# A two-layer vision tower on one Trainium2 core: the order of work where layer 1's attention begins and ends

## The chip, the cores and the metric

The kernel runs on one core of one Trainium2 chip. The core has five engines that take their instructions in order [...]: TensorE (PE, matrix products; its weight loads are shown apart as PEld), VectorE (DVE), ScalarE (ACT), GpSimd (POOL) and SyncE (SP, which here only issues DMA). The metric is the device time of one execution in microseconds (us), the median of several runs.

## The reference, cut to what matters

32 images of 256 tokens with 256 features go through a tokenizer and two layers. Layer 0 is a gated attention and a feed-forward that works only on the 127 best-ranked tokens of each image; layer 1 is the attention that the change is about, and a feed-forward with experts. All is float32.

```
h = tokenizer(x)
h = h + attn0(layernorm(h))                    # stage B of the kernel
x = layernorm(h)                               # stage C
w = x @ wr + br;  idx = the 127 largest of w;  h = h + x
h[idx] += w[idx] * (gelu(x[idx] @ w1 + b1) @ w2 + b2)
x = layernorm(h)                               # stage D
k = tanh(gelu(x @ Wk1 + bk1) @ Wk2 + bk2) * freq * pi    # phases; q likewise
r[i] = sum over j <= i of sum over phases of cos(k[j] - q[i]) * (x[j] @ Wv + bv)
h = h + x + layernorm(r / sqrt(64 * (i + 1))) @ Wo + bo
h = h + ffn1(layernorm(h))                     # stage E
```

## The kernel before, in words

`H` holds all 32 images in on-chip memory, two blocks of 128 tokens each. Every engine's instructions run in exactly the order in which the program writes them: a manual schedule covers PE, DVE, ACT, POOL and SP. So the Python loops below *are* the queues, and an instruction that waits holds all that is written after it on its engine. All matrix products go to one pool of eight PSUM banks (`bank()`), taken in turn; a bank can be taken again when its reader of eight allocations ago is done.

**Stage B** (layer 0's attention) ends with a step that makes the norms and ranking weights of images 28 and 29 (`norms_c`), turns the first quad's ranked tokens (`turn_c(0)`) and writes the last output (`output_b`, PE's rows `w_wo,gT`).

**Stage C** (layer 0's feed-forward, from line 847) goes by quads of four images. `step_c(t)` reads a table, `ORDER_C`: for a quad whose turn it is, `hidden_c` in two halves (rows `xsel,w_w`; ACT applies the gelu), `made` in two halves (rows `w_w,hT`; DVE adds a bias into `cy`, SP writes it to `results` in DRAM), `turn_c` of the next quad, and then for the quad that is done `fetch` (POOL: four indirect DMAs from `results` into `cx`, half a quad at a time) and `update` (DVE: `h<-cx,w_kept,h` at line 827 with new statistics, then a power on POOL). Which tokens are ranked is found by `ranks`: PE turns the weights (`turn_weights`, row `ident,cw`, line 482), DVE compares every weight with every other (lines 389 to 397), and POOL scatters the tokens to `ranked` in DRAM by their rank. The rankings of the last four images fall in steps 0 and 1 of stage C. There, PE's first product of step 1 stands behind a turn of weights that need `norms_c(B-2)`, which on DVE is written after `ranks(B-4)`.

**Stage D** (layer 1's attention, from line 873) goes by pairs of images; a pair is named by its first image. Step r of pair u runs at `t = 3u + r`:

- 0 `norm_d` (DVE, into `dx`; the first pair's norms, in `cx`, are made ahead, in stage C),
- 1 `turn` (PE transposes, ACT and DVE copy one half each into `dxT`) and `residual_d` (POOL, four adds of 128x512),
- 2 `hidden` twice (PE rows `dxT,w_wk` and `dxT,w_wq`; ACT gelu into `dg`),
- 3 `phases` (PE rows `dg`; ACT tanh; a chain on DVE: `dz` twice, `dn`, `dz`; ACT `Sin`). Gelu and `Sin` need different function tables of ACT, so each change costs a table load,
- 4 `match` (PE rows `dz`; DVE multiplies by the causal weights into `dat`),
- 5 `memory` (PE rows `dat`; ACT copies into `dm`),
- 6 `output` (PE rows `wvo,dm`, four banks; DVE statistics of each; `pow_rstd` on POOL),
- 7 `add_output` (DVE, line 952, waits for that power and frees the four banks) and `stats_e` (DVE, then a power on POOL).

So in a full round three pairs are under way, and the latency of one pair's chain is covered by PE work of the others. In the first round there is no other pair yet, and in the last none any more. The last quad's `fetch` and `update` of stage C (`step_c(32)` to `step_c(34)`) are written into stage D at t = 3, 4 and 5.

**Stage E** (layer 1's feed-forward, line 983 on) is a pipeline over images with a table of its own; the change doesn't touch it.

Of the kernel before, what the change touches and what calls it, by code (L numbers as in the profile page):

```python
# [33 lines left out]
F32 = mybir.dt.float32  # L34
# [6 lines left out]
P = 128  # L41
B, N, D = 32, 256, 256
NC = N // P
# [36 lines left out]
def vit_tower(tc, a, out):  # L80

    nc = tc.nc
    top = ExitStack()
    cpool = top.enter_context(tc.tile_pool(name="cpool", bufs=1))
    spool = top.enter_context(tc.tile_pool(name="spool", bufs=3))
# [59 lines left out]
    def pow_rstd(o, var):  # L145

        n = o.shape[1]
        nc.gpsimd.tensor_scalar(o, var, 1.0, 1e-5, ALU.mult, ALU.add)
        nc.gpsimd.tensor_tensor(o, o, minus_half[:, 0:n], ALU.pow)
# [52 lines left out]
    px = passing_x.enter_context(tc.tile_pool(name="c_x", bufs=1, reuse_waits="tile"))  # L202
# [69 lines left out]
    with (  # L272
# [7 lines left out]
        for k, n in enumerate(PARTS):  # L280
            f = sum(PARTS[:k])
# [68 lines left out]
        for b in range(B):  # L350
# [12 lines left out]
            if b in (B - 6, B - 4):  # L363
                u = (b - B + 6) // 2
# [39 lines left out]
    with (  # L404
# [71 lines left out]
        def turn_weights(b0):  # L476
            p = bank()
            for j in range(2):
                w = normed_c[b0][j][1]
                for c in range(NC):  # L480
                    o = j * N + c * P
                    nc.tensor.transpose(p[:, o : o + P], w[:, c : c + 1].to_broadcast([P, P]), ident)  # L482
            return p

        def ranks(b0, p):
            for j in range(2):
                rank_c(b0 + j, *normed_c[b0][j], p[:, j * N : (j + 1) * N])
# [54 lines left out]
    p2 = region_c.enter_context(tc.tile_pool(name="c_2", bufs=2, reuse_waits="tile"))  # L542
# [224 lines left out]
    def norm_d(b0, s, pool, name, bufs):  # L767
        s.xs = []
        for j in range(2):
            x = pool.tile([P, NC, D], F32, name=name, bufs=bufs)  # L770
            st, rs, i = at(st_d, b0 + j)
            q = slice(i * NC, (i + 1) * NC)
            one = spool.tile([P, NC], F32, name="d_one")
            nc.vector.scalar_tensor_tensor(one, st[:, i, :, 0], -1.0, rs[:, q], ALU.mult, ALU.mult)
            nc.vector.tensor_scalar(one, one, 1.0, None, ALU.add)
            for c in range(NC):
                nc.vector.tensor_scalar(
                    x[:, c, :], H[b0 + j][:, c, :], rs[:, i * NC + c : i * NC + c + 1], one[:, c : c + 1],
                    ALU.mult, ALU.add,
                )  # L780
            s.xs.append(x)

    def residual_d(b0, s):
        for j in range(2):
            h = H[b0 + j]
            nc.gpsimd.tensor_tensor(h, h, s.xs[j], ALU.add)
            nc.gpsimd.tensor_tensor(h, h, over(add_row, [P, NC, D], 1), ALU.add)

    with region_c:
        st_d = new_stats("d")  # L790

        def hidden_c(b0, s, half):
            if half == 0:
                s.hT = p2.tile([P, 8, 4 * P], F32, name="hT")
            for m in range(4 * half, 4 * half + 4):
                p = bank()
                for k in range(2):
                    mm(p, w1[:, k, m * P : (m + 1) * P], s.xsel[:, k, :], k == 0, k == 1)
                nc.scalar.activation(s.hT[:, m, :], p, AF.Gelu_apprx_tanh, bias=col("b1", m))

        def made(b0, s, half):
            for j in range(2 * half, 2 * half + 2):
                p = bank()
                for m in range(8):
                    mm(p[:, 0:D], s.hT[:, m, j * P : (j + 1) * P], w2[:, m, :], m == 0, m == 7)
                y = p2.tile([P, D], F32, name="cy", bufs=4)
                nc.vector.tensor_tensor(y, p[:, 0:D], row_c("b2"), ALU.add)
                nc.sync.dma_start(results[b0 + j][:], y)

        def fetch(b0, s, half):  # L810
            s.y = s.y if half else []
            for b in range(b0 + 2 * half, b0 + 2 * half + 2):
                y = px.tile([P, NC, D], F32, name="cx", bufs=8)
                for c in range(NC):
                    k = b * NC + c
                    nc.gpsimd.indirect_dma_start(
                        y[:, c, :], None, results[b][:], bass.IndirectOffsetOnAxis(rank_of[:, k : k + 1], 0)
                    )
                s.y.append(y)

        def update(b0, s, half):
            for j in range(2 * half, 2 * half + 2):
                b = b0 + j
                st, rs, i = at(st_d, b)
                for c in range(NC):
                    k = b * NC + c
                    nc.vector.scalar_tensor_tensor(
                        H[b][:, c, :], s.y[j][:, c, :], w_kept[:, k : k + 1], H[b][:, c, :], ALU.mult, ALU.add
                    )
                    stats(st, i, c, H[b][:, c, :])  # L830
            pow_rstd_of(st_d, b0 + 2 * half, 2)

        ORDER_C = ((0, hidden_c, 0), (1, hidden_c, 1), (2, made, 0), (-1, turn_c, 0), (-8, first_ranks, 0),
                   (3, made, 1), (4, fetch, 0), (5, fetch, 1), (5, update, 0), (6, update, 1))

        def step_c(t):
            for at_step, do, j in ORDER_C:
                u, r = divmod(t - at_step, 4)  # L840
                if r == 0 and 0 <= u < B // 4 and (u > 1 or do is not first_ranks):
                    do(4 * u, quads[u], j)

        END_C = 4 * (B // 4 - 1) + 4
        pairs = [Pair() for _ in range(B // 2)]
        preparing = prepare()
        for t in range(END_C):
            if t < 2:
                ranks(B - 4 + 2 * t, turn_weights(B - 4 + 2 * t))
            if t == 0:  # L850
                norms_c(B - 2)
                residuals_c(B - 2)
            if t == END_C - 2:
                norm_d(0, pairs[0], px, "cx", 8)
            step_c(t)
            if t >= 8:
                next(preparing, None)
        passing.close()
# [5 lines left out]
    with (  # L864
# [3 lines left out]
        def turn(b0, s):  # L868
            s.xT = p2.tile([P, 2, 2 * N], F32, name="dxT")
            transposed(s.xT, s.xs, copy_split)  # L870

        def hidden(b0, s, i):

            g = p2.tile([P, 2, 2 * N], F32, name=f"dg{i}")
            for m in range(2):
                p = bank()
                for k in range(2):
                    mm(p, (wk1, wq1)[i][:, k, m * P : (m + 1) * P], s.xT[:, k, :], k == 0, k == 1)
                nc.scalar.activation(g[:, m, :], p, AF.Gelu, bias=bias_d[:, 2 * i + m : 2 * i + m + 1])
            s.g = (s.g if i else []) + [g]  # L880

        def phases(b0, s):

# [48 lines left out]
                nc.scalar.copy(m.rearrange("p k n -> p (k n)"), p)  # L932
                s.m.append(m)

        def output(b0, s):
            st_m = spool.tile([P, 2 * NC, 2], F32, name="d_st")
            s.po = []
            for q in range(2 * NC):
                m, c, p = s.m[q // NC], q % NC, bank()
                for k in range(2):  # L940
                    mm(p, m[:, k, c * P : (c + 1) * P], wvo[:, k, :], k == 0, k == 1)
                six = spool.tile([P, 6], F32, name="six")
                nc.vector.bn_stats(six, p[:, 0:D])
                nc.vector.bn_aggr(st_m[:, q, :], six)
                s.po.append(p)
            s.rs = spool.tile([P, 2 * NC], F32, name="d_rs")
            pow_rstd(s.rs, st_m[:, :, 1])

        def add_output(b0, s):
            for q, p in enumerate(s.po):  # L950
                h = H[b0 + q // NC][:, q % NC, :]
                nc.vector.scalar_tensor_tensor(h, p[:, D:], s.rs[:, q : q + 1], h, ALU.mult, ALU.add)
# [6 lines left out]

        for t in range(3 * (B // 2 - 1) + 8):
            def do(step, which, *more):
                u, r = divmod(t - step, 3)
                if r == 0 and 0 <= u < B // 2:
                    which(2 * u, pairs[u], *more)

            do(1, turn)
            do(7, add_output)
            if t != 4:  # L970
                do(4, match)
            do(7, stats_e)
            do(1, residual_d)
            do(2, hidden, 0)
            if t == 5:
                match(0, pairs[0])
            do(2, hidden, 1)
            do(5, memory)
            do(3, phases)
            if t:  # L980
                do(0, norm_d, p8, "dx", 4)
            do(6, output)
            if 3 <= t <= 5:
                step_c(END_C + t - 3)
    right_d.close()
    passing_x.close()
    by_hand.close()
# [721 lines left out]
```

## Time and profile before

| | |
|---|---|
| time | 2002.92 us, median of 3 runs (2000.7 to 2003.91) |
| span of the profiled execution | 2000.3 us, 37646 instructions |
| mean granted TensorE clock | 0.984 |
| stage C from its first hidden product to its last `made` | 692.0 to 933.9 us |
| stage D | 933.9 to 1285.0 us |
| a full round of stage D | 21.0 us |
| stage E | 1285.0 us to the end |

Times in the profile count from the span's start. In a timeline row the columns are start, duration, engine, line, operation, output and inputs, how many were merged, and in square brackets the idle time of the engine before it and what ended it. A line can be that of a helper: L115 is every matrix product, L188 the transposes in `transposed`, L482 the turn of the ranking weights. In a table by windows each stretch gives its length, the busy time of PE, PEld, DVE, ACT and POOL with their number of instructions, the granted clock of PE as a share of full speed, the share of DMA, and GB/s. A profile doubles some records of float32 products, so counts are read only against each other.

### The profile page before, as it was taken

The numbers are of one execution on the slowest core, as the hardware profiler recorded it, in microseconds if no ns is written. First come the engines' busy times: TensorE is split into PE (matmuls) and PEld (weight loads), VectorE is DVE, ScalarE is ACT, GpSimd is POOL, SyncE is SP. The second block draws the span as 40 slices with busy tenths as digits, with TensorE's granted clock in tenths as the row PEclk, the third lists the DMA queues.
The fourth block names the chain that finished last, engine by engine and source line by source line (L and its number), as shares of the span: only waits on it lengthen the run. The fifth ranks groups of instructions, "written<-read, shape, count | busy, mean of one in ns | idle before, by whom it ended". The sixth has DMA issues, their size and how long they took to land.

```text
span 2000.3 us, 37646 instructions
## 1 busy us (share of the span) xinstructions
PE 1942.6 (97%) x15108; PEld 1373.5 (69%) x15108; DVE 1289.7 (64%) x3605; ACT 824.6 (41%) x1549; POOL 722.7 (36%) x692
## 2 busy tenths in 40 slices
PE   9999999999999999998999999999999999999984
PEld 7886676666767666765555555577777777777762
DVE  2334566656565735334655646567889998989986
ACT  0002222222121111122344444377777777777761
POOL 1223234334342334234333342214443444444353
PEclk9999999999999999999999999999999999999995
DMA  8540000000000232121000000001222121212211
GB/s 297 158 142 1 0 19 29 24 14 22 11 21 11 85 98 80 52 68 50 11 1 1 0 1 1 6 18 44 49 53 57 44 65 44 60 49 58 52 50 54
DMA packets 69812, 95.08 MB, mean 48 GB/s; under 512 B 8576, under 2 KB 51200, under 8 KB 69248
## 3 DMA queue, kind: packets, MB, share of 16 engines
q1 hardware_dynamic: 62912, 75.04, 13.2%
q0 software_dynamic: 6144, 16.79, 2.7%
q8 instruction: 121, 1.98, 0.4%
q10 hardware_dynamic: 576, 0.79, 0.1%
q14 instruction: 59, 0.48, 0.1%
HBM read 46.45 MB, written 20.97 MB: 34 GB/s over the span
## 4 chain that ended last, share of the span: by engine, by line
PE 94%; DVE 4%; DMA 1%; ACT 0%; issue 0%; SPq 0%; POOL 0%; ACTq 0%; DVEq 0%
PE bank L115 89%; PE bank L750 2%; PE bank L188 1%; PE bank L1254 1%; DMA both<-hx 0%; DMA patch<-in_patches_dram 0%; PE bank L229 0%; PE bank L482 0%; DVE fout L1263 0%; DVE ctmp L375 0%; DVE two L1185 0%; DVE fout L1259 0%; DVE ctmp L391 0%; DVE ctmp L389 0%; DVE six L123 0%
## 5 line engine op out<-in xcount | busy, mean ns | idle before, releaser
L1102 ACT ACTIVATE et<-bank 128x512 f32<-128x512 f32 x384 | 202.4, 599 | 59.0 <-DVE bank L1100 58.5
L115 PEld LDWEIGHTS bank<-ev,et 128*64 128x64 f32 x6144 | 198.2, 137 | 33.2 <-ACT et L1102 20.6
L115 PE MATMUL bank<-ev,et 128*64 128x74 f32 (+1 forms) x6144 | 211.1, 226 | 0.0
L1100 DVE TENSOR_TENSOR bank<-bank,w_tri 128x256 f32<-128x256 f32 (+1 forms) x384 | 173.3, 514 | 56.1 <-PE bank L115 54.4
L1180 POOL TENSOR_TENSOR eo<-eo,gate 128x1024 f32<-128x1024 f32 x64 | 121.9, 1926 | 215.9 <-DVE gate L1177 203.2
L115 PE MATMUL bank<-g,sx 64*128 64x512 f32 (+1 forms) x512 | 191.0, 502 | 1.4 <-ACT g L1060 1.4
L115 PE MATMUL bank<-g,sw 64*128 64x512 f32 (+1 forms) x512 | 189.9, 502 | 0.1
L115 PE MATMUL bank<-tokW,patch 128*128 128x256 f32 x768 | 166.7, 380 | 2.8 <-DMA patch<-in_patches_dram 2.8
L115 PEld LDWEIGHTS bank<-tokW,patch 128*128 128x128 f32 x768 | 146.0, 190 | 23.8 <-DMA tokW<-in_tokW_dram 3.3
L115 PE MATMUL bank<-bxT,w_wuv 128*128 128x512 f32 x300 | 131.4, 592 | 0.0
L1132 POOL TENSOR_TENSOR hv<-hv,minus_half 128x8 f32<-128x8 f32 x64 | 119.5, 1868 | 5.3
L1118 ACT COPY eo<-bank 128x286 f32<-128x286 f32 x256 | 97.4, 423 | 57.9 <-PE bank L115 51.4
L115 PE MATMUL bank<-wvo,dm 128*128 128x512 f32 x256 | 114.0, 598 | 0.0
L115 PE MATMUL bank<-w_wo,gT 128*128 128x256 f32 x512 | 113.1, 379 | 0.0
L115 PE MATMUL bank<-xsel,w_w 128*128 128x512 f32 x256 | 113.1, 600 | 0.0
L115 PE MATMUL bank<-attn,bv 128*128 128x256 f32 x512 | 113.1, 379 | 0.0
L115 PE MATMUL bank<-w_w,hT 128*128 128x256 f32 x512 | 113.1, 379 | 0.0
L115 PEld LDWEIGHTS bank<-attn,bv 128*128 128x128 f32 x512 | 97.2, 190 | 19.6 <-issue 6.9
L123 DVE BATCH_NORM_STATS2 six<-h 128x6 f32<-128x256 f32 x256 | 105.5, 412 | 4.4
L1131 POOL TENSOR_SCALAR hv<-ranges 128x8 f32<-128x8 f32 x64 | 39.1, 611 | 190.1 <-DVE ranges L1193 189.9
L115 PEld LDWEIGHTS bank<-w_w,hT 128*128 128x128 f32 x512 | 96.7, 190 | 15.8 <-issue 3.4
L115 PEld LDWEIGHTS bank<-w_wo,gT 128*128 128x128 f32 x512 | 97.2, 190 | 13.2
(265 smaller groups left out, 3739.0 us busy)
## 6 DMA issues: line engine op xcount, KB each, us to landing
patch<-in_patches_dram SPq DMA_DIRECT2D x31, 768.0 KB
sw<-sx SPq DMA_DIRECT2D x64, 128.0 KB
both<-fxT SPq DMA_DIRECT2D x64, 128.0 KB
both<-hx SPq DMA_DIRECT2D x64, 128.0 KB
out_dram<-fout SPq DMA_DIRECT2D x32, 256.0 KB
cs<-ranked SPq DMA_DIRECT2D x32, 128.0 KB
results<-cy SPq DMA_DIRECT2D x32, 128.0 KB
w_w<-in_w_dram SPq DMA_DIRECT2D x2, 1024.0 KB
```

The source lines that it names most:

```text
L115: nc.tensor.matmul(o, lhsT, rhs, start=first, stop=last)
L123: nc.vector.bn_stats(six, x)
L188: nc.tensor.transpose(p[:, o : o + P], x[:, c, k * P : (k + 1) * P], ident)
L750: nc.tensor.transpose(p[:, o : o + P], x[:, c, k * P : (k + 1) * P], ident)
L1100: nc.vector.tensor_tensor(own, own, over(tri, [P, n_e, P], 1), ALU.add)
L1102: nc.scalar.activation(t, p, AF.Exp)
L1118: nc.scalar.copy(im.o[:, c * NH + n, 0:OC], p[:, 0:OC])
L1131: nc.gpsimd.tensor_scalar(v, x, 1.0 / HD, 1e-8, ALU.mult, ALU.add)
L1132: nc.gpsimd.tensor_tensor(v, v, minus_half, ALU.pow)
L1180: nc.gpsimd.tensor_tensor(im.mix[k], im.mix[k], over(im.gate[:, :, 2 * k : 2 * k + 2], [P, NC * NH, 2, HD], 3), ALU.mult)
L1254: nc.tensor.transpose(im.po[:, o : o + P], im.fT[:, k, c * P : (c + 1) * P], ident)
```

## The change

Three edits of order, at three places; no instruction is added or taken away.

1. *Rankings of the last four images.* In steps 0 and 1 of stage C the feed-forward's products (`step_c`) are written ahead of `ranks` and its turn of weights, so that PE has work while DVE makes norms and rankings.
2. *The start of layer 1's attention.* The second pair's `norm_d` is made together with the first's, in stage C, and its `turn` right after the first pair's hidden layers (t = 2). The first `match` moves between the two halves of the second pair's second hidden layer, so that it comes later on PE. The second pair's residual adds move to t = 5, and the last quad's `fetch` and `update` from t = 3, 4, 5 to t = 6, 7, 8.
3. *The end of layer 1's attention.* At t = 48 only three of the four products of the last but one pair's `output` are written; the last pair's `match` follows, then the fourth product and `add_output`. So the last `dat` stands ahead of the fourth statistics and of `add_output` on DVE, and PE has a product to do while DVE makes it.

```diff
         for t in range(END_C):
-            if t < 2:
-                ranks(B - 4 + 2 * t, turn_weights(B - 4 + 2 * t))
             if t == 0:
                 norms_c(B - 2)
                 residuals_c(B - 2)
             if t == END_C - 2:
-                norm_d(0, pairs[0], px, "cx", 8)
+                for u in range(2):
+                    norm_d(2 * u, pairs[u], px, "cx", 8)
             step_c(t)
+            if t < 2:
+                ranks(B - 4 + 2 * t, turn_weights(B - 4 + 2 * t))
...
-        for t in range(3 * (B // 2 - 1) + 8):
+        NP = B // 2
+        for t in range(3 * (NP - 1) + 8):
...
-            do(1, turn)
-            do(7, add_output)
+            last = t == 3 * NP + 1
+            if t != 4:
+                do(1, turn)
+            if not last:
+                do(7, add_output)
             if t != 4:
                 do(4, match)
+            if last:
+                output(B - 4, pairs[NP - 2], (3,))
+                add_output(B - 4, pairs[NP - 2])
             do(7, stats_e)
-            do(1, residual_d)
+            if t != 4:
+                do(1, residual_d)
             do(2, hidden, 0)
-            if t == 5:
+            if t == 2:
+                do(2, hidden, 1)
+                turn(2, pairs[1])
+            elif t == 5:
+                do(2, hidden, 1, (0,))
                 match(0, pairs[0])
-            do(2, hidden, 1)
+                do(2, hidden, 1, (1,))
+            else:
+                do(2, hidden, 1)
             do(5, memory)
             do(3, phases)
-            if t:
+            if t == 5:
+                residual_d(2, pairs[1])
+            if t > 3:
                 do(0, norm_d, p8, "dx", 4)
-            do(6, output)
-            if 3 <= t <= 5:
-                step_c(END_C + t - 3)
+            if t == 3 * NP:
+                output(B - 4, pairs[NP - 2], (0, 1, 2))
+            else:
+                do(6, output)
+            if 6 <= t <= 8:
+                step_c(END_C + t - 6)
```

`hidden` and `output` take a list of the parts to write, so that one call can be split in two.

More of the change, by code (lines that the diff above doesn't have):

```diff
@@ L870, in turn, with hidden @@
             transposed(s.xT, s.xs, copy_split)
-        def hidden(b0, s, i):
-            g = p2.tile([P, 2, 2 * N], F32, name=f"dg{i}")
-            for m in range(2):
+        def hidden(b0, s, i, ms=(0, 1)):
+            if ms[0] == 0:
+                s.g = (s.g if i else []) + [p2.tile([P, 2, 2 * N], F32, name=f"dg{i}")]
+            g = s.g[i]
+            for m in ms:
                 p = bank()
@@ L879, in hidden @@
                 nc.scalar.activation(g[:, m, :], p, AF.Gelu, bias=bias_d[:, 2 * i + m : 2 * i + m + 1])
-            s.g = (s.g if i else []) + [g]
         def phases(b0, s):
@@ L933, in memory, with output @@
                 s.m.append(m)
[L935 to L938, printed above, removed]
+        def output(b0, s, qs=range(2 * NC)):
+            if qs[0] == 0:
+                s.st, s.po = spool.tile([P, 2 * NC, 2], F32, name="d_st"), []
+            for q in qs:
                 m, c, p = s.m[q // NC], q % NC, bank()
@@ L943, in output @@
                 nc.vector.bn_stats(six, p[:, 0:D])
-                nc.vector.bn_aggr(st_m[:, q, :], six)
+                nc.vector.bn_aggr(s.st[:, q, :], six)
                 s.po.append(p)
-            s.rs = spool.tile([P, 2 * NC], F32, name="d_rs")
-            pow_rstd(s.rs, st_m[:, :, 1])
+            if len(s.po) == 2 * NC:
+                s.rs = spool.tile([P, 2 * NC], F32, name="d_rs")
+                pow_rstd(s.rs, s.st[:, :, 1])
         def add_output(b0, s):
@@ L958, in stats_e @@
             pow_rstd_of(st_e, b0, 2)
-        for t in range(3 * (B // 2 - 1) + 8):
+        NP = B // 2
+        for t in range(3 * (NP - 1) + 8):
             def do(step, which, *more):
                 u, r = divmod(t - step, 3)
-                if r == 0 and 0 <= u < B // 2:
+                if r == 0 and 0 <= u < NP:
                     which(2 * u, pairs[u], *more)
-            do(1, turn)
-            do(7, add_output)
+            last = t == 3 * NP + 1
[3 more added lines that the diff above has]
+                do(7, add_output)
             if t != 4:
                 do(4, match)
+            if last:
+                output(B - 4, pairs[NP - 2], (3,))
+                add_output(B - 4, pairs[NP - 2])
             do(7, stats_e)
-            do(1, residual_d)
+            if t != 4:
+                do(1, residual_d)
             do(2, hidden, 0)
-            if t == 5:
+            if t == 2:
[3 more added lines that the diff above has]
+                do(2, hidden, 1, (0,))
                 match(0, pairs[0])
-            do(2, hidden, 1)
+                do(2, hidden, 1, (1,))
+            else:
+                do(2, hidden, 1)
             do(5, memory)
             do(3, phases)
-            if t:
+            if t == 5:
+                residual_d(2, pairs[1])
+            if t > 3:
                 do(0, norm_d, p8, "dx", 4)
-            do(6, output)
-            if 3 <= t <= 5:
-                step_c(END_C + t - 3)
+            if t == 3 * NP:
[4 more added lines that the diff above has]
+                step_c(END_C + t - 6)
     right_d.close()
```

## The prediction

> **What bounds the kernel now.** I read the engine totals and the chain of the page first, then the chain in order of time around the third part of the span, then the windows and the timelines of PE, POOL and DVE there. Engine totals and chain shares:
>
> ```profile
> PE 1942.6 (97%) x15108; PEld 1373.5 (69%) x15108; DVE 1289.7 (64%) x3605; ACT 824.6 (41%) x1549; POOL 722.7 (36%) x692
> ...
> PE 94%; DVE 4%; DMA 1%; ACT 0%; issue 0%; SPq 0%; POOL 0%; ACTq 0%; DVEq 0%
> ```
>
> TensorE bounds it, so an edit pays only where PE stands still. The windows say where (PE busy, then the others, granted clock, DMA):
>
> ```profile
> 690.00:700.00 10.00, 9.03 (x27) 4.38 (x26) 9.48 (x32) 2.75 (x4) 3.95 (x6) 1.00 0.70 208
> 700.00:720.00 20.00, 17.30 (x62) 11.27 (x63) 10.58 (x35) 3.23 (x5) 10.45 (x11) 0.91 0.42 134
> 720.00:930.00 210.00, 210.00 (x827) 143.26 (x826) 83.98 (x260) 42.58 (x64) 69.90 (x92) 1.00 0.22 66
> ...
> 945.00:960.00 15.00, 8.94 (x32) 4.83 (x32) 11.96 (x25) 5.62 (x7) 9.06 (x9) 0.66 0.10 27
> 960.00:980.00 20.00, 20.00 (x90) 11.37 (x89) 14.46 (x41) 7.86 (x11) 3.44 (x5) 1.00 0.03 8
> 980.00:1260.00 280.00, 280.00 (x1170) 157.27 (x1169) 157.43 (x464) 119.79 (x161) 99.92 (x108) 1.00 0.00 1
> ...
> 1270.00:1280.00 10.00, 7.23 (x35) 5.51 (x32) 5.20 (x18) 1.17 (x2) 2.41 (x4) 0.83 0.00 0
> ```
>
> Three holes, each followed by a lowered clock, and full stretches between them. PE's timeline shows what each waits for:
>
> ```profile
> 701.60 0.40 PE L482 MATMUL bank<-ident,cw 128*128 128x128 f32 x2 [2.54 <-DVE cw L378]
> 703.10 0.43 PE L482 MATMUL bank<-ident,cw 128*128 128x128 f32 x2 [1.09 <-DVE cw L378]
> 703.37 8.73 PE L115 MATMUL bank<-xsel,w_w 128*128 128x512 f32 x16
> ...
> 948.70 0.80 PE L188 MATMUL bank<-ident,dx 128*128 128x128 f32 x2 [4.57 <-DVE dx L777]
> 951.86 1.65 PE L188 MATMUL bank<-ident,dx 128*128 128x128 f32 x6 [2.35 <-DVE dx L777]
> 953.33 5.38 PE L115 MATMUL bank<-dxT,w_wk 128*128 128x512 f32 x8
> ...
> 1273.76 4.55 PE L115 MATMUL bank<-dat,dx 128*128 128x256 f32 x16 [2.77 <-DVE dat L919]
> ```
>
> Without the slow clock the same rows last 7.03, 3.70 and 2.78 us (at 692.03, 960.15, 984.69): each hole costs its idle time and some 1.7 us more, the second also 1.0 in its transposes. The edit aims at just these three.
>
> [...] the trace shows POOL and DVE in the written order throughout. [...] a `d_one` of 0.17 us took 1.26 beside a POOL add at 949.06. [...] a fetch whose issue ended at 908.41 let DVE go on at 910.50, 2.1 us later.
>
> **The change, part by part.** All times are on the clock of the old trace. A pair of images is named by its first image: pair 2 is the second, pair 6 the fourth.
>
> *Rankings.* Before, PE turned the weights of images 30 and 31 only after `norms_c(B-2)`, which queued on DVE behind `ranks` of 28. Now the feed-forward's first hidden half runs ahead of the first turn of weights, the second half ahead of the second. PE is done with the previous stage at 691.35; two halves of 6.87 (32 rows last 13.74, 726.62 to 740.36) and two turns of 0.44 end at 705.97, where `made` began at 711.93: 5.96 us saved. DVE does the norms from 696.7 (after POOL's power, 695.64 + 1.04) for 3.3, the two rankings for 4.6 each, with up to 2.5 of blocking by POOL's two adds: finished by 711.7. Only `cy` waits there, and the banks concerned are not wanted before about 713. The scatters end later, but quad 7 is read 18 steps on. Cost nothing.
>
> *Start of layer 1's attention.* Pair 2's norms (2.0 us) move into stage C, where DVE is idle 7.01 us before 923.69: free. Its residual adds on POOL (5.2) follow those of pair 0 at 938.4, where POOL has nothing else: free. From 942.19, where the first pair's hidden layers end, PE then runs, at the durations of an undisturbed round: turn 0.97, phases 1.88 (to 945.04), hidden(2) 3.49 + 1.74 (to 950.27), match 1.51, the last hidden product 1.74, memory 2.71 (to 956.23), phases 1.88, output at 958.11. Its one wait is `Sin`: tanh starts 1.99 after the phases and `Sin` ends 4.84 later (944.18 to 949.02 before), so 949.99, just ahead of match at 950.27. The hidden gelus stand on ACT behind `Sin` and a 1.28 table load, to 953.3; the last, whose product ends at 953.5, goes out at 954.3, and its reader starts at 956.23. Eight banks are enough. Output began at 968.28: 10.17 saved, holes and slow clock together.
>
> *Last quad's fetches, from t = 3..5 to t = 6..8: where some of it goes again.* On POOL the first four fetches now stand behind `pow_rstd` of output(0), and the last four behind pair 0's `stats_e` power and the four residual adds of pair 4. On DVE the last update now stands ahead of the `dz` chain of pair 4 and the norms of pair 6: both queue behind it, and PE waits for those norms at turn(6). The rows that price this queue are these, of POOL and DVE:
>
> ```profile
> 982.66 0.19 POOL L148 TENSOR_SCALAR rs_e<-st_e 128x4 f32<-128x4 f32 x1 [4.84 <-DVE st_e L124]
> ...
> 983.91 1.26 POOL L786 TENSOR_TENSOR h<-h,dx 128x512 f32<-128x512 f32 x1
> ...
> 987.82 1.27 POOL L787 TENSOR_TENSOR h<-h,add_row 128x512 f32<-128x512 f32 x1
> ...
> 990.34 0.88 DVE L899 TENSOR_SCALAR dz<-dturn,cols 128x512 f32<-128x512 f32 x2 [7.77 <-ACT dturn L897]
> ...
> 994.70 0.73 DVE L777 TENSOR_SCALAR dx<-h,rs_d,d_one 128x256 f32<-128x256 f32 x2
> ```
>
> In that round output starts at 989.28 and its power ends at 998.98, 9.70 later; so here at 967.81. Four fetches (4.83, as from 938.48) end 972.8; the `stats_e` power and start-up 1.25; the adds 5.18 (983.91 to 989.09), to 979.3; four more fetches (4.73, with 0.15 ahead) end 984.2; landing 2.1 later, 986.3; the last update part 1.08 (913.15 to 914.23): DVE is free at 987.4. `dz` to the last `dx` takes 5.09 (990.34 to 995.43): 992.5. PE wants these for turn(6) at 958.11 + 7.06 (output) + 0.97 + 1.51 + 6.97 + 2.71 + 1.88 + 7.06 = 986.27. A new hole of 6.2 us, between the old ones in length, with 1.7 to 2.7 of slow clock; I take 2.0. Of 10.17 some 1.95 stay. Update 0 is done before, even if DVE is blocked through the adds (982.1), and the adds keep their 1.27 wherever the trace shows such blocking. Update work itself (12 instructions, 4.2 us, each) fits the 7.77 idle.
>
> *End.* At t = 48 three output groups (5.30) follow 1262.35, match at 1267.65 (its `Sin` ended at 1267.36) to 1269.16, the fourth group 1.76 to 1270.92. `dat` now stands ahead of the statistics on DVE and is ready at 1270.5, before PE reaches memory. Memory to 1273.63; output(30) there, for its first bank is free at 1273.6: fourth statistics 1271.75, power 1.3, one add 0.41. It began at 1278.15: 4.5 saved. The margins here are 0.1 to 0.4 us. The later layer begins that much sooner in the same order.
>
> Sum: 5.96 + 1.95 + 4.5 = 12.4; 2002.92 - 12.4 = 1990.5.
>
> **Rivals.** *No new hole.* For it: an in-order wait may be shorter than worked, and DVE idles 7.8 us a round. Against: the POOL queue is a plain sum of seen durations, and it overruns by 6. It gives 5.96 + 10.17 + 4.5 = 20.6: 1982.3. *A deeper hole.* Residual adds and update 0 share DVE's and POOL's path; if POOL yields too, its adds lengthen by up to the update's 4.2, and the slow clock takes 2.7: 2002.92 - 12.4 + 4.9 = 1995.4, and up to 1999 if one of the small margins fails as well. Against: in the old trace DVE waited, never POOL. *Slower.* If the deferred fetches went one at a time as the scatters on `ranked` do (4.23 us wait at 703.00 instead of the 0.30 between fetches) the second four would end 4 x 3.9 = 15.7 later; with a yielding POOL 4.2 and 0.7 of clock: 1990.5 + 20.6 = 2011. Against: fetches write separate halves of a tile and went out 1.27 apart.
>
> **How the numbers follow.** New hole as worked 0.60; none 0.20; deeper 0.16, of which 0.03 within 0.2% (4.0 us); slower 0.04. So faster 0.93, same 0.03, slower 0.04. The range runs from the no-hole case, 1981.5, to the deeper one, 1995.5, and leaves out little over one in ten for the ends, plus my own errors.
>
> **What would show it.** Right: the three holes gone (hidden, phases and memory products follow each other without idle), and one new hole of about 6 us ahead of pair 6's transposes (`bank<-ident,dx`), released by DVE `dx`, with DVE's `h<-cx,w_kept,h` waiting on the fetch into `cx` just before. Wrong: that hole missing (time near 1982), or PE stalls on `dz` in match, or on a bank in the last output.

## The result, and the profile after

| | before, on the same chip | after |
|---|---|---|
| time | 2001.81 us (2000.3 to 2003.91) | 1990.07 us (1989.0 to 1990.42) |
| ratio | 1 | 0.994 (95%: 0.9922 to 0.9957) |
| span of the profiled execution | 2000.3 us | 1988.2 us |
| mean granted TensorE clock | 0.984 | 0.985 |

The changed kernel takes 11.7 us less. It was run a second time beside the experiments at the end: 1989.65 us, ratio 0.9945 (0.9931 to 0.9958). The forecast was 1990.5.

The page's engine totals and the engine shares of its chain, for the kernel after:

```profile
PE 1939.9 (98%) x15108; PEld 1374.1 (69%) x15108; DVE 1286.7 (65%) x3605; ACT 823.1 (41%) x1549; POOL 724.2 (36%) x692
...
PE 94%; DVE 3%; DMA 1%; POOL 1%; issue 0%; ACT 0%; SPq 0%; POOLq 0%; ACTq 0%; DVEq 0%
```

Instruction counts are the same on all engines, and PE's busy time fell by only 2.7 us: the rest of the gain is idle time. DVE's share of the chain fell by a point and POOL's rose from 0% to 1%, which is where to look for something new. The windows (length, busy time of PE, PEld, DVE, ACT and POOL, granted clock, DMA share, GB/s) of the kernel after:

```profile
690.00:700.00 10.00, 10.00 (x31) 5.04 (x30) 8.28 (x22) 2.75 (x4) 4.11 (x6) 1.00 0.72 220
700.00:720.00 20.00, 20.00 (x88) 15.42 (x87) 12.65 (x46) 3.33 (x5) 8.36 (x9) 1.00 0.41 135
...
945.00:960.00 15.00, 15.00 (x72) 8.73 (x70) 7.81 (x23) 7.27 (x11) 0.00 (x0) 1.00 0.00 1
...
980.00:990.00 10.00, 4.64 (x20) 3.39 (x22) 8.49 (x26) 2.93 (x3) 2.65 (x4) 0.70 0.00 0
...
1260.00:1270.00 10.00, 10.00 (x47) 6.26 (x44) 7.20 (x25) 1.17 (x2) 2.02 (x4) 1.00 0.00 0
```

The three windows that had holes are full, at full clock. A new one, from 980 to 990, has PE busy for 4.64 of 10 us at a clock of 0.70. PE's timeline of the kernel after shows the same places row by row:

```profile
697.80 0.60 PE L482 MATMUL bank<-ident,cw 128*128 128x128 f32 x4
698.24 7.03 PE L115 MATMUL bank<-xsel,w_w 128*128 128x512 f32 x16
...
972.82 7.13 PE L115 MATMUL bank<-wvo,dm 128*128 128x512 f32 x16
985.12 0.80 PE L188 MATMUL bank<-ident,dx 128*128 128x128 f32 x2 [5.16 <-DVE dx L777]
986.16 1.65 PE L188 MATMUL bank<-ident,dx 128*128 128x128 f32 x6 [0.24 <-DVE dx L777]
987.74 2.93 PE L115 MATMUL bank<-dz 64*128 64x256 f32 x16
990.60 3.76 PE L115 MATMUL bank<-dxT,w_wk 128*128 128x512 f32 x8
...
1261.14 1.98 PE L115 MATMUL bank<-wvo,dm 128*128 128x512 f32 x4
1262.96 2.78 PE L115 MATMUL bank<-dat,dx 128*128 128x256 f32 x16
```

Rows without brackets follow without idle time. The turns of ranking weights and the last memory product no longer wait, and the hidden half behind the first turn takes 7.03 instead of 8.73. Before pair 6's transposes PE waits for DVE's `dx`, and match behind them takes 2.93 where an undisturbed one takes 1.58 (at 943.90). DVE's timeline tells what `dx` waited for:

```profile
971.20 0.18 DVE L124 BATCH_NORM_AGGREGATE st_d<-six 128x2 f32<-128x6 f32 x1
976.62 0.48 DVE L827 SCALAR_TENSOR_TENSOR h<-cx,w_kept,h 128x256 f32<-128x256 f32 x1 [5.24 <-DMA cx<-results,rank_of]
...
980.42 0.48 DVE L827 SCALAR_TENSOR_TENSOR h<-cx,w_kept,h 128x256 f32<-128x256 f32 x1 [0.26 <-DMA cx<-results,rank_of]
...
981.50 0.85 DVE L901 TENSOR_SCALAR dz<-dturn,cols 128x512 f32<-128x512 f32 x2
...
985.69 0.73 DVE L777 TENSOR_SCALAR dx<-h,rs_d,d_one 128x256 f32<-128x256 f32 x2
```

For 5.24 us DVE stands at the head of its queue on a token fetch, with `dz` and `dx` written behind it. And POOL's timeline tells why the fetch is so late:

```profile
961.54 1.06 POOL L816 DMA_INDIRECT cx<-results,rank_of  x1 [0.18 <-issue]
...
966.72 1.04 POOL L149 TENSOR_TENSOR rs_e<-rs_e,minus_half 128x4 f32<-128x4 f32 x1
967.75 1.25 POOL L786 TENSOR_TENSOR h<-h,dx 128x512 f32<-128x512 f32 x1
...
971.90 1.27 POOL L787 TENSOR_TENSOR h<-h,add_row 128x512 f32<-128x512 f32 x1
973.34 1.05 POOL L816 DMA_INDIRECT cx<-results,rank_of  x1 [0.16 <-issue]
...
977.23 0.96 POOL L816 DMA_INDIRECT cx<-results,rank_of  x1 [0.30 <-issue]
```

From 961.5 to 978.2 POOL has no gap longer than 0.30: four fetches, a power, four residual adds, four fetches. That is the queue the prediction added up.

### The profile page after: what moved, and what is told of

Same layout as the page of the kernel before. It is cut to its first block, busy times and chain, and to the rows that moved or that the text cites. A ratio compares the mean times of both kernels' runs of the same rounds, so it can differ in the third digit from the quotient of the medians.

```text
span 1988.2 us, 37643 instructions
## 1 busy us (share of the span) xinstructions
PE 1939.9 (98%) x15108; PEld 1374.1 (69%) x15108; DVE 1286.7 (65%) x3605; ACT 823.1 (41%) x1549; POOL 724.2 (36%) x692
## 4 chain that ended last, share of the span: by engine, by line
PE 94%; DVE 3%; DMA 1%; POOL 1%; issue 0%; ACT 0%; SPq 0%; POOLq 0%; ACTq 0%; DVEq 0%
PE bank L115 89%; PE bank L750 3%; PE bank L188 1%; PE bank L1276 1%; DMA both<-hx 0%; PE bank L229 0%; PE bank L482 0%; POOL cx L816 0%; DMA patch<-in_patches_dram 0%; DVE fout L1285 0%; DVE fout L1281 0%; DVE two L1207 0%; DMA cx<-results,rank_of 0%; DVE enorm L1256 0%; DVE er L1209 0%
```

## The experiments

To tell the parts apart better than device times can, each run is also read on PE's own timeline between six marks: the end of stage B, the first `made` product (`w_w,hT`), the first transpose of stage D, the first output product of pair 0, the first hidden product of pair 6, and the first transpose of stage E. All values are us from mark to mark; the stretch from `made` to the first transpose, which the table leaves out, is 221.91 or 221.92 in every run.

| kernel | stage B's end to `made` | turn(0) to output(0) | output(0) to hidden(6) | hidden(6) to stage E | stage B's end to stage E |
|---|---|---|---|---|---|
| before | 20.58 | 34.43 | 30.45 | 286.29 | 593.67 |
| before, again | 18.90 | 33.64 | 30.45 | 286.09 | 590.99 |
| after | 14.61 | 24.35 | 38.79 | 281.84 | 581.51 |
| after, again | 14.61 | 24.35 | 38.34 | 281.78 | 581.00 |
| rankings alone | 14.61 | 33.96 | 30.45 | 286.24 | 587.17 |
| end alone | 20.62 | 34.12 | 30.45 | 281.79 | 588.89 |
| start alone | 21.51 | 24.35 | 38.93 | 284.84 | 591.55 |
| start alone, again | 20.60 | 24.35 | 38.86 | 284.68 | 590.40 |
| `dat` ahead, no filler | 14.61 | 24.36 | 38.71 | 282.50 | 582.09 |
| fetches at t = 3, 4, 5 | 14.61 | 26.21 | 30.45 | 281.78 | 574.97 |
| fetches at t = 3, 5, 8 | 14.61 | 26.06 | 30.46 | 281.78 | 574.83 |
| adds behind the fetches | 14.61 | 24.36 | 35.57 | 282.01 | 578.46 |
| last update at t = 11 | 14.61 | 24.35 | 30.46 | 281.78 | 573.12 |
| last update at t = 11, again | 14.61 | 24.36 | 30.45 | 281.78 | 573.12 |

The theory: three independent savings on PE's path, of 5.96, 10.17 and 4.5 us, and a new wait of 8.2 that takes the place of most of the second, because DVE's queue has the last update ahead of pair 6's norms. The rivals: the savings aren't additive, or belong to other edits; the new wait comes from POOL or from the later fetches as such, and not from DVE's order.

### Each edit alone

Rankings: the kernel before, with the first edit alone.

```diff
         for t in range(END_C):
-            if t < 2:
-                ranks(B - 4 + 2 * t, turn_weights(B - 4 + 2 * t))
             ...
             step_c(t)
+            if t < 2:
+                ranks(B - 4 + 2 * t, turn_weights(B - 4 + 2 * t))
```

> The kernel before with only the first edit: the feed-forward's first products ahead of the last rankings. Theory: the hole at 699 to 703 and its lowered clock go, nothing else moves: 6.0 us faster than before, and PE's first made product 6.0 us earlier. Rival (DVE is as full there as PE: it only passes the wait on to cy and from there to a bank): 2 to 3 us faster, a wait on DVE cy or on a bank near 713 to 720.

Measured: 1996.22 us against 2001.24 of the kernel before, ratio 0.9972 (0.9963 to 0.9981). On PE's path `made` comes 5.97 us sooner (20.58 to 14.61) and after it nothing differs by more than 0.47 us, where the two runs of the kernel before differ by 0.79. The saving is there and belongs to this edit.

End: the kernel before, with the third edit alone.

```diff
+            last = t == 3 * NP + 1
             do(1, turn)
-            do(7, add_output)
+            if not last:
+                do(7, add_output)
             if t != 4:
                 do(4, match)
+            if last:
+                output(B - 4, pairs[NP - 2], (3,))
+                add_output(B - 4, pairs[NP - 2])
...
-            do(6, output)
+            if t == 3 * NP:
+                output(B - 4, pairs[NP - 2], (0, 1, 2))
+            else:
+                do(6, output)
```

> The kernel before with only the third edit: three of the last but one pair's outputs, match, the fourth. Theory: memory of the last pair follows without idle, 4.5 us faster than before. Rival (the wait moves to the last output's first bank, which add_output frees): 2 us faster, a wait on DVE h (line 955) before the last output.

Measured: 1996.72 us against 2001.24, ratio 0.9982 (0.9973 to 0.9991). From hidden(6) to stage E it takes 281.79 instead of 286.29: 4.50 us, with the rest of the path as before.

Start: the kernel before, with the second edit alone (both pairs' norms in stage C, pair 2's turn at t = 2 and its residual adds at t = 5, match between the hidden halves, fetches and updates at t = 6, 7, 8).

```diff
-                norm_d(0, pairs[0], px, "cx", 8)
+                for u in range(2):
+                    norm_d(2 * u, pairs[u], px, "cx", 8)
...
+            if t == 2:
+                do(2, hidden, 1)
+                turn(2, pairs[1])
+            elif t == 5:
+                do(2, hidden, 1, (0,))
                 match(0, pairs[0])
-            do(2, hidden, 1)
+                do(2, hidden, 1, (1,))
...
-            if 3 <= t <= 5:
-                step_c(END_C + t - 3)
+            if 6 <= t <= 8:
+                step_c(END_C + t - 6)
```

> The kernel before with only the second edit: pair 2 normed and turned with pair 0, fetches and updates at t = 6 to 8. Theory: the hole at 944 to 952 goes (10.2 us), the new one before pair 6's transposes comes (8.3 us): 1.9 us faster than before. Rival (the new hole depends on the other edits): 8 to 10 us faster.

Measured: 1999.46 us against 2001.24, ratio 0.9995 (0.9986 to 1.0003), so the device time alone can't tell the largest edit from no change. The path can: output(0) comes 10.08 us sooner after turn(0), and from there to hidden(6) 8.48 us are given back. PE's timeline of this kernel has the hole of the kernel after, with none of the other edits in it:

```profile
979.52 7.13 PE L115 MATMUL bank<-wvo,dm 128*128 128x512 f32 x16
991.95 0.80 PE L188 MATMUL bank<-ident,dx 128*128 128x128 f32 x2 [5.30 <-DVE dx L777]
993.00 1.65 PE L188 MATMUL bank<-ident,dx 128*128 128x128 f32 x6 [0.24 <-DVE dx L777]
994.58 2.93 PE L115 MATMUL bank<-dz 64*128 64x256 f32 x16
...
1272.69 2.88 PE L115 MATMUL bank<-dat,dx 128*128 128x256 f32 x16 [2.77 <-DVE dat L921]
```

5.30 idle instead of 5.16, and behind it the same 0.80, 1.65 and 2.93. The hole belongs to the second edit. The last line is of interest further down. The three edits alone save 5.0, 4.5 and 1.8 us of device time, 11.3 together, against 11.7 of the whole: they add up.

### What the new hole comes from

First, the kernel after with the last quad's fetches and updates back where they were.

```diff
-            if 6 <= t <= 8:
-                step_c(END_C + t - 6)
+            if 3 <= t <= 5:
+                step_c(END_C + t - 3)
```

> The changed kernel with fetches and updates at t = 3, 4 and 5, where the kernel before had them. Theory: the hole before pair 6's transposes goes (8.3 us), but update 0 now stands on DVE ahead of the first dat, with POOL's residual adds of pair 2 beside it, and update 1 ahead of pair 2's dz chain: PE waits 1 to 3 us for dat or for pair 2's phases chain. 17 to 19.5 us faster than the kernel before. Rival (the updates must be kept out of the first round, where they cost as much as they do at t = 6 to 8): no faster than the changed kernel, 12 us faster than the kernel before.

Measured: 1981.82 us against 1999.93 of the kernel before, ratio 0.991 (0.9893 to 0.9926). The hole is gone (30.45 from output(0) to hidden(6)), but 1.86 us are lost ahead of output(0). PE's timeline of this kernel:

```profile
944.59 1.58 PE L115 MATMUL bank<-dz 64*128 64x256 f32 x16 [1.43 <-ACT dz L906]
```

The loss has the size that was expected, 1 to 3 us, but most of it lies at another place than the one expected. Match of pair 0 begins 1.5 us late (the rest falls at the memory products after it). It waits for `Sin`, because the chain in front of it began late, on ACT's timeline:

```profile
939.70 0.84 ACT L899 ACTIVATE dturn<-bank,cols 128x256 f32<-128x256 f32 x2 [3.44 <-PE bank L115]
```

This tanh began 3.84 us after the phases' products, where the kernels before and after take 1.99. What held it the trace doesn't name, and no run here settles it.

Next, the fetches apart from the wait for them: fetches of the first half at t = 3, those of the second half and the first update at t = 5, the last update at t = 8.

```diff
-            if 6 <= t <= 8:
-                step_c(END_C + t - 6)
+            if t in (3, 5, 8):
+                step_c(END_C + (3, 5, 8).index(t))
```

> The changed kernel with the last quad's fetch 0, fetch 1 with update 0, and update 1 written at t = 3, 5 and 8 instead of 6, 7 and 8. Theory (POOL's queue makes the second fetch late, DVE's last update holds the norms of pair 6, PE waits): POOL has both fetches out by about 941 and 947 on the changed trace's clock, no DVE wait on the fetch into cx ahead of the last update, no hole before pair 6's transposes; 8.3 us faster than the changed kernel, about 20 us faster than the kernel before. Rival (DVE simply has too much work at t = 7 to 9, wherever the fetches stand): update 1 still stands in that slot, the hole shrinks by no more than half, 4 us or less faster than the changed kernel.

Measured: 1983.18 us against 1999.93, ratio 0.9916 (0.9899 to 0.9932). The hole is gone again, and 1.71 us are lost ahead of output(0), this time for a reason that DVE's timeline shows:

```profile
939.18 2.94 DVE L901 TENSOR_SCALAR dz<-dturn,cols 128x512 f32<-128x512 f32 x2 [2.07 <-ACT dturn L899]
```

It is not the moved operation that costs, but the one it displaces: with four fetches ahead of them on POOL, pair 2's residual adds now run from 936.58 to 941.83, beside this `dz`, which takes 2.94 instead of 0.88. So the fetches of the second half can go out earlier, but the first half's place at t = 3 has a price of its own. The last update still stands at t = 8 here, and PE has no hole behind it, though update 0 has left t = 7. What both would cost in their old places without a wait can be estimated from the rows of the kernel after: there PE's hole is 6.37 us (worked out further down), and DVE waits 5.57 for fetches in its last update (5.24, 0.07 and 0.26), so the work itself would make 0.8 of the hole at most. Little is left of the rival that DVE simply has too much to do.

The decisive one leaves the fetches of the kernel after where they are, and moves only the last update, on DVE with its power on POOL, three steps on.

```diff
-            if 6 <= t <= 8:
-                step_c(END_C + t - 6)
+            if t in (6, 7, 11):
+                step_c(END_C + (6, 7, 11).index(t))
```

> The changed kernel with only the last update (DVE, and its power on POOL) moved from t = 8 to t = 11; both fetches stay where they are on POOL, as late as before. Theory (the late fetch hurts only because DVE takes instructions in order and the update stands ahead of pair 4's dz and pair 6's norms): the hole goes, 8.3 us faster than the changed kernel, about 20 us faster than the kernel before, although the fetches land at the same time. Rival (POOL's lateness itself delays something PE needs, such as the power of an output): the hole stays, no faster than the changed kernel.

Measured: 1982.05 us against 1999.93, ratio 0.9906 (0.9889 to 0.9922). The last fetch on POOL's timeline is as late as before (its issue ends at 980.80; on this trace all of stage D is 1.95 later than in the kernel after, where it ended at 978.19):

```profile
979.85 0.95 POOL L816 DMA_INDIRECT cx<-results,rank_of  x1 [0.31 <-issue]
```

Yet DVE makes `dz` and the norms without waiting for it:

```profile
975.82 0.88 DVE L901 TENSOR_SCALAR dz<-dturn,cols 128x512 f32<-128x512 f32 x2 [2.49 <-ACT dturn L899]
...
980.28 0.95 DVE L777 TENSOR_SCALAR dx<-h,rs_d,d_one 128x256 f32<-128x256 f32 x2
...
989.43 0.45 DVE L827 SCALAR_TENSOR_TENSOR h<-cx,w_kept,h 128x256 f32<-128x256 f32 x1
```

and PE's timeline has no idle time there:

```profile
974.77 7.13 PE L115 MATMUL bank<-wvo,dm 128*128 128x512 f32 x16
981.74 1.04 PE L188 MATMUL bank<-ident,dx 128*128 128x128 f32 x8
982.71 1.58 PE L115 MATMUL bank<-dz 64*128 64x256 f32 x16
984.22 3.70 PE L115 MATMUL bank<-dxT,w_wk 128*128 128x512 f32 x8
```

DVE now waits for ACT's tanh, which is the chain's own latency, and the update finds its data there at 989.43 when it is due. So the cause is the order on DVE. That the fetches are late costs nothing by itself. The saving against the kernel before is 17.9 us here, less than the 20 expected, for the kernel before came out at 1999.93 there; beside 2001.67, further down, it is 20.4.

Last, POOL's part of the queue: the kernel after, with pair 4's residual adds behind the second four fetches.

```diff
-            if t != 4:
+            if t not in (4, 7):
                 do(1, residual_d)
...
             if 6 <= t <= 8:
                 step_c(END_C + t - 6)
+            if t == 7:
+                residual_d(4, pairs[2])
```

> The changed kernel with only the four residual adds of pair 4 moved on POOL from ahead of the second four fetches to behind them and the power of update 0. Theory: the second fetches go out 5.2 us earlier, DVE's wait on cx shrinks by that; but the adds then run beside pair 4's dz chain on DVE and slow it by 1 to 3 us. The hole before pair 6's transposes falls from 5.2 us to 1 to 3, with less or no lowered clock: 4 to 7 us faster than the changed kernel. Rival (DVE's own work makes the hole): unchanged, within 1 us of the changed kernel.

Measured: 1987.84 us against 1999.93, ratio 0.9935 (0.9918 to 0.9951). The interval overlaps that of the kernel after (0.9922 to 0.9957), so the device time doesn't tell the two apart; on PE's path it is 3.05 us better, less than the 4 to 7 expected. DVE's timeline shows both halves of it:

```profile
974.69 0.48 DVE L827 SCALAR_TENSOR_TENSOR h<-cx,w_kept,h 128x256 f32<-128x256 f32 x1 [0.87 <-DMA cx<-results,rank_of]
...
980.04 2.22 DVE L901 TENSOR_SCALAR dz<-dturn,cols 128x512 f32<-128x512 f32 x2
982.29 1.64 DVE L904 TENSOR_SCALAR dn<-dz 128x1024 f32<-128x1024 f32 x1
```

The wait on `cx` shrank from 5.24 to 0.87 (and 0.17 and 0.38 further on), as expected, since the fetches no longer stand behind the adds. But the adds then run from 977.86 to 983.38 beside `dz` and `dn`, which take 2.22 and 1.64 instead of 0.85 and 0.69: 2.3 us, within the 1 to 3 that the expectation gave them. The hole on PE's timeline has the length that was expected too, 1 to 3 us:

```profile
985.97 0.65 PE L188 MATMUL bank<-ident,dx 128*128 128x128 f32 x2 [2.51 <-DVE dx L777]
987.01 1.09 PE L188 MATMUL bank<-ident,dx 128*128 128x128 f32 x6 [0.39 <-DVE dx L777]
988.03 2.93 PE L115 MATMUL bank<-dz 64*128 64x256 f32 x16
```

What the expectation had wrong is the clock: match behind this shorter hole takes 2.93, as behind the longer one.

### The end: which part of the edit does it

The kernel after, with all four output products of the last but one pair ahead of match as before, but `dat` still ahead of `add_output` on DVE.

```diff
             if last:
-                output(B - 4, pairs[NP - 2], (3,))
                 add_output(B - 4, pairs[NP - 2])
...
             if t == 3 * NP:
-                output(B - 4, pairs[NP - 2], (0, 1, 2))
+                output(B - 4, pairs[NP - 2], (0, 1, 2, 3))
```

> The changed kernel with all four of the last but one pair's outputs ahead of the last match on PE, as before; add_output still stands behind dat on DVE. It tells the order on DVE from the filler on PE. Theory: DVE makes dat right after match, but PE has nothing until then: a hole of 1.0 to 1.5 us before memory, [...] so 1.0 to 1.5 us slower than the changed kernel (3.0 to 3.5 of the 4.5 kept). Rival (the clock falls after any wait there): 3 us slower than the changed kernel, memory's 16 products at 4.5 us instead of 2.8.

Measured: 1990.34 us against 2001.24, ratio 0.9953 (0.9937 to 0.997). The last memory product on PE's timeline of this kernel:

```profile
1263.02 2.88 PE L115 MATMUL bank<-dat,dx 128*128 128x256 f32 x16 [0.64 <-DVE dat L921]
```

A hole of 0.64 is left, smaller than the 1.0 to 1.5 expected, and the product behind it took 2.88, where one without a hole takes 2.78 and that of the kernel before took 4.55; what the clock does behind a hole of 1.0 to 1.5 was therefore not tested. So of some 4.5 us the order of `dat` and `add_output` on DVE brings 3.8 (286.29 to 282.50), and the fourth product kept back on PE, with its statistics on DVE, the other 0.7 (282.50 to 281.84).

### The best of them, once more, and what repeats

The kernel after, the one with the last update at t = 11, the one with the start alone and the kernel before, all on one chip.

> The changed kernel with the last update at t = 11, beside the changed kernel itself on one chip. Theory: the hole of the changed kernel and its lowered clock are all that stands between them, 8.3 us: 0.4% faster than the changed kernel, 20 us faster than the kernel before. Rival (part of the difference seen between chips was the chip): 0.1 to 0.2%.

> The changed kernel, unaltered, beside the one with the late update. Theory: 12 us faster than the kernel before; the hole before pair 6's transposes again 5 to 6 us long, and PE's rows after it slow by some 2 us more, but how much of the lowered clock falls on them may differ from the first profile. Rival (the lowered clock follows a hole of that length in a fixed way): the same rows and durations as in the first profile within 0.1 us.

> The second edit alone, looked at again for the lowered clock only. In its first profile the hole of 2.77 us before the last memory products was followed by no slow rows (2.88 us), in the kernel before the same hole by slow ones (4.55). Theory [...]: in a second profile one or more of the three holes' slow parts differ by over 0.3 us from the first one. Rival (the kernel's own order decides it): the same durations again.

> The kernel before, looked at again for the lowered clock only. Theory: the idle parts of its three holes come again within 0.1 us, but the slow rows after them (8.73, 5.38 and 4.55 us in the first profile against 7.03, 3.70 and 2.78 undisturbed) change by over 0.3 us in at least one place. Rival: the same durations again.

Measured, against 2001.67 of the kernel before: last update at t = 11 1981.24 us, ratio 0.9898 (0.9883 to 0.9913); the kernel after 1989.65 us, ratio 0.9945 (0.9931 to 0.9958); start alone 1998.52 and the kernel before 2000.98, one run each. The intervals of the first two don't meet: moving one update three steps on makes the changed kernel 8.4 us faster, and 20.4 faster than the kernel before. The marks of all four repeat to within 0.5 us, except where the clock behaved otherwise. The kernel before, again, on PE's timeline:

```profile
703.31 0.40 PE L482 MATMUL bank<-ident,cw 128*128 128x128 f32 x2 [2.54 <-DVE cw L378]
704.81 0.43 PE L482 MATMUL bank<-ident,cw 128*128 128x128 f32 x2 [1.10 <-DVE ctmp L375]
705.08 7.03 PE L115 MATMUL bank<-xsel,w_w 128*128 128x512 f32 x16
```

The holes are those of the first trace, 2.54 and 1.10, but the hidden half behind them took 7.03, not 8.73. The kernel after, again:

```profile
985.74 0.80 PE L188 MATMUL bank<-ident,dx 128*128 128x128 f32 x2 [5.19 <-DVE dx L777]
...
988.37 2.45 PE L115 MATMUL bank<-dz 64*128 64x256 f32 x16
```

Its hole is the same too (5.19 against 5.16), and match behind it took 2.45, not 2.93. So in both kernels the rival of a fixed price falls. In the start alone only the first of its three holes behaved otherwise (9.41 us the first time, 8.73 the second); behind the other two match took 2.93 both times, the hidden products next to it 3.91 and 3.76, and the last memory product 2.88 and 2.89.

## Why the prediction was right, point by point

**Rankings.** Forecast 5.96 us, measured 5.97 against the trace that the forecast was worked from; the stretch took 14.61 in every run with this edit. Against the other traces without it (18.90 to 21.51) the saving is 4.3 to 6.9, because the slow clock behind the old hole varies. What was costed at nothing was nothing. On this trace's clock, 0.42 ahead of the old one here, DVE's norms began at 696.55 (forecast 696.3), two of their products took 1.48 instead of 0.42 beside POOL's adds (2.1 us more together, where the forecast allowed up to 2.5), and the last ranking ended at 711.36 (forecast 711.3); `cy` began as it ended, and PE did not wait.

**Start.** Forecast 10.17 us, measured 10.08, again against the trace that the forecast was worked from; against the three other traces with the old start (33.64 to 34.12) it is 9.3 to 9.8. The one tight place, `Sin` ahead of match by 0.28 us, held: match ran from 943.90 without idle time. That this margin was real, two experiments showed by breaking it: 1.43 and 1.64 us of wait as soon as tanh or `dz` came late.

**Fetches.** This was the step that decided the forecast, and it is the one to check number by number. The forecast stood on the clock of the old trace; in the kernel after the same work comes 6.39 us sooner (5.97 of it the rankings; the other 0.42 was there at the end of stage B, ahead of any edit).

| event | forecast, less 6.39 | measured |
|---|---|---|
| output(0) starts | 951.72 | 951.81 |
| its power ends on POOL | 961.42 | 961.37 |
| first four fetches issued | 966.4 | 966.37 |
| residual adds of pair 4 end | 972.9 | 973.17 |
| second four fetches issued | 977.8 | 978.19 |
| DVE free of the last update | 981.0 | 981.50 |
| last `dx` | 986.1 | 986.42 |
| PE wants turn(6) | 979.88 | 979.79 |
| PE's hole | 6.2 | 6.37, to 986.16: 5.40 idle, with two transposes in it |
| slow clock after it | 2.0 | 1.96 |

PE's wish is 972.82 plus 6.97, the length of the output before it. The hole and its clock delay hidden(6) by 8.34 us, against 8.2. That the clock's part met the 2.0 so closely is luck: the forecast took it out of a range of 1.7 to 2.7, and in the second profile of the same kernel it was 1.5. The drift in the rows before comes from POOL's adds, at up to 1.45 instead of 1.27 beside the update, and from the period of the fetches. That it is DVE's order that turns a late fetch into a PE hole was only argued in the forecast; the run with the last update at t = 11 shows it.

**End.** Forecast 4.5 us, measured 4.45 in the whole and 4.50 alone. The margins of 0.1 to 0.4 us held: rows from 1259.63 to 1272.44 follow without idle time. What the forecast treated as one thing are two, 3.8 from DVE's order and 0.7 from PE's. And its size has a condition the forecast didn't see: where the old hole left the clock alone, as in the two runs of the start alone (284.84 and 284.68 from hidden(6) to stage E, against 281.8), the edit would bring only 2.9 to 3.1.

**Sum.** 5.97 + 10.08 - 8.34 + 4.45 = 12.16 us up to stage E, against 12.4 forecast. Two of the forecast's own sums are a tenth off, without effect: by its terms the residual adds end at 979.2, not 979.3, and the last output's first bank is free at 1273.5, not 1273.6. Stage E itself took 715.8 us, 0.5 more than before (715.3), and the spans differ by 12.1. The device time came out at 1990.07, 0.4 under the forecast. That closeness is in part luck: the forecast took the 12.4 from 2002.92, while the kernel before came out at 2001.81 beside the kernel after, so the saving was 11.7, and the two differences, 1.1 and 0.7, partly cancel. Both are less than the spread of the kernel before (2000.3 to 2003.91). What the runs confirm is the path and its waits, not tenths of a microsecond in the total.

**The rivals.** *No new hole* (1982.3) did not happen, but the experiments that take the hole away arrive there: 1981.2 to 1983.2, two of them with a loss of 1.7 to 1.9 elsewhere. So that case was priced rightly to within the scatter, and it is what the change could have been. *A deeper hole* asked for POOL to yield to DVE through its adds, by up to 4.2 us: they took 5.42 instead of 5.18, while DVE's update rows took 1.16 and 0.81 instead of 0.45. It was again DVE that lost most. *Slower* asked for fetches one at a time: the second four went out from 973.34 to 978.19, some 1.27 apart.

## What to carry to other kernels

In these queues, which run in order (DVE's `dz` stood behind a 5.24 us wait for a fetch), the place of a consumer mattered more than that of its transfer: a late fetch cost nothing, but its consumer written one chain too early cost TensorE 8.3 us, and moving that consumer three steps on gave them back. So when an edit defers a producer, walk down the queue of the engine that consumes it and ask what stands behind the wait; that sum, made from row durations, was right to 0.2 us here. And split a change by its parts before judging it: the largest saving (10.1 us) was invisible in the device time because the same edit gave 8.5 us back.

## What the runs showed of the hardware that was not expected

**The clock drop is not a fixed price of a hole.** The same hole, in the same program, was followed by slow rows in one execution and not in another. Behind 2.5 and 1.1 us of idle time 16 hidden rows took 8.73 in the kernel before and 7.03 in the kernel before, again; in the start alone they took 9.41 (behind 2.55 and 0.84) and 8.73 (behind 2.54 and 1.09). Behind 2.77 us the last memory product took 4.55 and 4.35 in the two runs of the kernel before, and 2.88 and 2.89 in the start alone (its line is shown above); without a hole it took 2.78. At that hole each program repeated itself; whether the program decides there, by what came before, no run here shows. The rows named thus took 0 to 2.4 us more than undisturbed, and the two traces of the kernel before differ by 1.7 us between two marks (20.58 and 18.90) for this alone. No run here shows why a hole is followed by slow rows one time and not another. Only hole lengths that happened to occur were seen; the shortest that matters was not looked for.

**Some DVE operations took longer beside POOL's adds, and others did not.** Beside POOL's 128x512 adds `dz` took 2.94 instead of 0.88 for two, `dn` 1.64 instead of 0.69, `h<-cx,w_kept,h` up to 1.16 instead of 0.45. The statistics between them, `six<-h`, kept their 0.43. POOL's own adds grew from 1.27 to at most 1.46. What sets the two kinds of DVE operation apart no run here shows. In the kernel after, with POOL's adds close behind each other, it was mostly DVE that lost: 1.07 us on two update rows, against 0.24 on the four adds. It cost PE 1.7 us in one experiment and DVE 2.3 in another, so the place of such adds on POOL belongs in the sum for DVE's chain.
